# Self-attention of a decoder: the causal mask of the scores by query goes from TensorE into VectorE's maximum

## The chip, the cores and the metric

The kernel runs on one core of a Trainium2 chip. Its time is the device time of one execution in microseconds. The engines are named as in the profile: PE is TensorE (PEld its weight loads), DVE VectorE, ACT ScalarE, POOL GpSimd, SP SyncE. DVE, ACT and PE reach PSUM[...].

## The reference

A decoder of two layers over x of shape (4, 512, 512): in each layer a self-attention, a cross-attention (in the second layer, a mix with a learned adjacency) and a feed-forward part, each with a residual and a layer norm after it. The change lies in the two self-attentions, 16 heads of 32:

```python
scores = jnp.einsum('bhqd,bhkd->bhqk', q, k) * scale
causal = jnp.tril(jnp.ones((S, S), dtype=bool))
scores = jnp.where(causal, scores, jnp.float32(-jnp.inf))
attn = jax.nn.softmax(scores, axis=-1)
out = jnp.einsum('bhqk,bhkd->bhqd', attn, v)
```

## The kernel before

The program runs in stages: the self-attention of layer 0 (to about 640 us of the span), the cross-attention with the quantisation of the weights behind it, the feed-forward part of layer 0, the self-attention of layer 1 (about 1490 to 2110 us), the adjacency and the experts.

**Two sets of scores.** `self_attention` works on groups n of four heads: 4 batches x 4 groups = 16 a layer. It forms the scores twice. `maxima` (L226) has queries on the partitions: for one block of 128 queries, i, and each of the four heads r, PE multiplies the queries with the first m = i + 1 blocks of keys (L237), four heads side by side on their own 32 rows of the array. The last block of keys is the one on the diagonal, and there PE adds the causal mask by a second product, the 128 x 128 bf16 mask times the identity, into the same PSUM tile (L243). DVE then takes the maximum of two heads in one instruction and writes it negated into `st` (L245). `parts` (L250) splits the negated maxima into three bf16 pieces in `pm`; `least` (L258) turns them over on PE (the rows `tp<-ident,pm`) and ACT copies them out. `softmax` (L270) has keys on the partitions: PE forms the scores again, adds the negated maxima with `pick` and the mask (rows `sc<-ident,mask`, L289, which the change leaves alone), and ACT takes the exponential. `values` (L294) sums the exponentials with `ones` (tile `tp`), multiplies them with the values (tile `mm`), and DVE forms four reciprocals `u` (L312) and the product `oT` (L313). `output` (L315) multiplies with Wo, and DVE adds it to x and normalises (L327 to L340).

**The loop** (L356) has 64 + 6 steps a layer. Step t = 4n + m calls, in this order: `maxima(n, 3 - m)`, so that the widths are 512, 384, 256 and 128 columns at m = 0, 1, 2, 3; `least` of the group before at m = 0; the first half of a dense piece (a projection of the next batch: q at m = 2, k at m = 3, v at m = 0); the `softmax` of five steps earlier; the second half of the dense piece. At m = 1 the dense piece is `values` and comes whole behind the softmax. In the last batch, from step 54, there are no projections left. `output` of a finished batch runs in four pieces over the following steps, and one step of the background (the selection of the adjacency: DVE, ACT, POOL and a little of PE) is put in at the end of each.

**What sets the order.** PE's matmuls of the attention are chained in program order by `in_order` (L395); a scheduler places all else on each engine when the program is built. So PE stands still when the next product of the chain isn't free to run. What frees it are PSUM tiles: `psum(3, 1, 1)` gives three pairs of banks for scores, one `tp` and one `mm`. `maxima` takes two pairs (heads 0 and 1, heads 2 and 3), `softmax` two more, from a ring of three. So the second pair of a softmax is the first pair of the maxima of the same step, and its products wait until DVE has read heads 0 and 1. The one `mm` tile goes from projection to projection and to `values`: the k products wait until DVE has read qT out of it (L214), the v products for ACT's kT (L218), the q products at m = 2 for oT.

Of the kernel before, what the change touches and what calls it, by code (L numbers as in the profile page):

```python
# [13 lines left out]
F32 = mybir.dt.float32  # L14
BF16 = mybir.dt.bfloat16
U32 = mybir.dt.uint32
AF = mybir.ActivationFunctionType
ALU = mybir.AluOpType
AX = mybir.AxisListType
PSUM = bass.MemoryType.PSUM  # L20

P = 128
B, S, D = 4, 512, 512
NT = S // P
# [4 lines left out]
NEG = -1e30  # L29
LOWEST = -3.4028235e38  # L30
# [10 lines left out]
def decoder_kernel(ctx: ExitStack, tc: tile.TileContext, a: dict, out: bass.AP):  # L41
    nc = tc.nc
    V, A, G, T = nc.vector, nc.scalar, nc.gpsimd, nc.tensor
# [14 lines left out]
    def psum_pair():  # L58
        return ps["sc"].tile([P, 2, 512], F32, tag="sc", name="sc")

    def psum_tp(dt=F32, n=4):
        return ps["tp"].tile([P, n, P], dt, tag="tp", name="tp")

    def psum_mm():
        return ps["mm"].tile([P, 512], F32, tag="mm", name="mm")
# [4 lines left out]
    ident16 = const.tile([P, P], BF16, tag="ident16", name="ident16")  # L70
    make_identity(nc, ident16)
    mask16 = const.tile([P, P], BF16, tag="mask16", name="mask16")
# [63 lines left out]
    def self_attention(pre, first, background=lambda: None):  # L136
        HD, NG, NJ = 32, 4, 4
        scale = 1.0 / math.sqrt(HD)
        multiply, transpose = in_order()
        with tc.tile_pool(name=pre + "w", bufs=1) as wp, tc.tile_pool(  # L140
            name=pre + "qkv", bufs=2
# [21 lines left out]
                G.memset(pick[32 * r : 32 * r + 3, r, :], 1.0)  # L163

            PM = []
            VA = []
            for k in range(2):
                t = wp.tile([P, NT, NJ, 32], BF16, tag=f"pm{k}", name=f"pm{k}")
                G.memset(t, 0.0)
                PM.append(t)  # L170
                t = wp.tile([P, NT, 4 * NG, HD], F32, tag=f"va{k}", name=f"va{k}")
                VA.append(t)
            XT, Q, K, ST, NM, O = {}, {}, {}, {}, {}, {}
# [19 lines left out]
            def project(b, f, k):  # L193
# [25 lines left out]
                else:  # L219
                    V.tensor_tensor(  # L220
                        VA[b % 2][:, f], pp.rearrange("p (h e) -> p h e", e=HD),
                        bias["v"].rearrange("p (h e) -> p h e", e=HD), ALU.add,
# [3 lines left out]
            def maxima(n, i):  # L226

                b, g = divmod(n, NG)
                if n not in ST:
                    ST[n] = po.tile([P, NT, NJ], F32, tag="st", name="st")  # L230
                st = ST[n]
                m = i + 1
                sc = [psum_pair() for _ in range(NJ // 2)]
                at = [sc[r // 2][:, r % 2, : m * P] for r in range(NJ)]
                for r in range(NJ):
                    rows = slice(HD * r, HD * (r + 1))
                    multiply(  # L237
                        at[r], Q[b][rows, g, ts(i, P)], K[b][rows, g, : m * P],
                        start=True, stop=False,
                    )  # L240
                for r in range(NJ):

                    multiply(at[r][:, i * P :], ident16, mask16, start=False, stop=True)  # L243
                for h in range(NJ // 2):
                    V.tensor_reduce(  # L245
                        st[:, i, 2 * h : 2 * h + 2], sc[h][:, :, : m * P], AX.X, ALU.max,
                        negate=True,
                    )

            def parts(n):  # L250
                st, pm = ST[n], PM[n % 2]
                rest = po.tile([P, NT, NJ], F32, tag="rest", name="rest")
                V.tensor_copy(pm[:, :, :, 0], st)
                V.tensor_tensor(rest, st, pm[:, :, :, 0], ALU.subtract)
                V.tensor_copy(pm[:, :, :, 1], rest)
                V.tensor_tensor(pm[:, :, :, 2], rest, pm[:, :, :, 1], ALU.subtract)

            def least(n):  # L258

                tp = psum_tp(BF16)  # L260
                for i in range(NT):
                    transpose(
                        tp[:, i, :], PM[n % 2][:, i].rearrange("p j e -> p (j e)"), ident16
                    )
# [29 lines left out]
            def values(n):  # L294

                b, g = divmod(n, NG)
                o, t = psum_mm(), psum_tp().rearrange("p n t -> p (n t)")
                for to, left in ((t, None), (o, VA[b % 2])):
                    for kb in range(NT):
# [15 lines left out]
            def output(b):  # L315

                x = X[b]
                st = small.tile([P, NT, 6], F32, tag="bst", name="bst")
                mv = small.tile([P, NT, 2], F32, tag="bmv", name="bmv")
                for i in range(NT):  # L320
                    pw = psum_tp().rearrange("p n t -> p (n t)")
                    for c in range(NK):
                        multiply(
                            pw, O[b][:, c, ts(i, P)], w["o"][:, c, :],
                            start=(c == 0), stop=(c == NK - 1),
                        )
                    V.tensor_tensor(x[:, i, :], pw, x[:, i, :], ALU.add)  # L327
                    V.bn_stats(st[:, i, :], x[:, i, :])
                    V.bn_aggr(mv[:, i, :], st[:, i, :])
                    if i < NT - 1:  # L330
                        yield
                sd = small.tile([P, NT], F32, tag="bsd", name="bsd")
                A.activation(sd, mv[:, :, 1], AF.Sqrt, bias=eps_t)
                rs = small.tile([P, NT], F32, tag="brs", name="brs")
                V.reciprocal(rs, sd)
                for i in range(NT):
                    V.tensor_scalar(
                        x[:, i, :], x[:, i, :], mv[:, i, 0:1], rs[:, i : i + 1],
                        ALU.subtract, ALU.mult,
                    )  # L340
                    yield
# [13 lines left out]
            late = iter(())  # L355
            for t in range(NT * total + 6):  # L356
                n, m = divmod(t, NT)
                k = t - 5
                if n < total:
                    maxima(n, NT - 1 - m)  # L360
# [26 lines left out]
                if m == NT - 1 and n < total:  # L387
                    parts(n)
                if m == 1 and n > 1 and (n - 2) % NG == NG - 1:
                    late = output((n - 2) // NG)  # L390
# [4 lines left out]
    def in_order():  # L395

        last = []

        def pinned(op):
            def call(*args, **kw):  # L400
                ins = op(*args, **kw)  # L401
                if last:
                    tc.add_manual_dep(ins.ins, last[0].name, ORDER, reason="in_order")
                last[:] = [ins.ins]

            return call

        return pinned(T.matmul), pinned(T.transpose)
# [42 lines left out]
    def cross_attention(background):  # L451
        HD, NG, NJ, NP = XD, XG, 4, XP
        multiply, transpose = in_order()
        with tc.tile_pool(name="ck", bufs=1) as kp, tc.tile_pool(
# [6 lines left out]
            G.memset(zero, 0.0)  # L461
            KS, KL, VA, XL = [], [], [], []
            for k in range(2):
# [3 lines left out]
                V.memset(t, 1.0)  # L467
                VA.append(t)
            for k in range(3):
# [4 lines left out]
            def load(b):  # L474
# [6 lines left out]
                G.tensor_copy(  # L481
                    VA[b % 2][:, :, :, :HD], cv.rearrange("p t (g e) -> p t g e", e=HD)
                )
# [891 lines left out]
    with tc.tile_pool(name="sims", bufs=1) as mp:  # L1375
        selection, background = selecting((0, 1), mp, split_context(mp))
        with psum(3, 1, 1):
            self_attention("L0", True, background)
            for _ in selection:
                pass  # L1380
# [17 lines left out]
    with tc.tile_pool(name="sims2", bufs=1) as mp:  # L1398
        selection, background = selecting((2, 3), mp)
        with psum(3, 1, 1):  # L1400
            self_attention("L1", False, background)
            for _ in selection:
                pass
# [49 lines left out]
```

## Time and profile before

| what | number |
| --- | --- |
| time, median of 3 runs | 2757.82 us (2756.66 to 2757.9) |
| the profiled execution's own time | 2759.02 us |
| its span, first to last instruction | 2757.3 us |
| granted TensorE clock, mean over the span | 0.951 |
| PE busy | 2393.0 us, 87% of the span |
| DVE busy | 1412.4 us, 51% |
| ACT busy | 1092.1 us, 40% |
| mask products by query (L243; the row is L401 `sc<-mask,ident`) | 512, mean 228 ns, 52.9 us in all |
| reductions (L245), 1024 / 768 / 512 / 256 elements | 64 of each, mean 1216 / 949 / 682 / 413 ns |
| oT (L313) | 32, mean 690 ns |

A line of the page or of a list names the kernel's line, the engine, the operation, the tile written and those read, partitions x elements, the count, the busy time and the mean of one; behind the second bar stands the engine's idle time ahead of these instructions and what ended it. All products of the attentions carry L401, the line of `in_order`, so they are told apart by their tiles: `sc<-kT,qT` in 32 rows is a score product of `maxima`, `sc<-qT,kT` one of `softmax`. Durations of matmuls overlap, since PE is pipelined; the distance from start to start is what counts.

### The profile page before, as it was taken

How to read it: one execution, taken by the hardware profiler on the slowest of the kernel's cores; microseconds unless marked ns; L12 is line 12 of the kernel's file. 1: busy time of each engine (PE TensorE's matmuls, PEld its weight loads, DVE VectorE, ACT ScalarE, POOL GpSimd, SP SyncE). 2: the span in 40 equal slices, each digit the busy share in tenths (PEclk: the TensorE clock that was granted, in tenths of full speed). 3: DMA queues.
4: the chain of work that ended last, by engine and by line, in shares of the span. 5: the costliest groups of instructions: out<-in, count | busy, mean ns of one | idle time of the engine just before them, and what ended most of it. 6: DMA issues, size and time to landing. Idle time of an engine off the chain costs nothing. (4 is left out here: it accounts for less than half of the span.)

```text
span 2757.3 us, 34743 instructions
## 1 busy us (share of the span) xinstructions
PE 2393.0 (87%) x13465; PEld 1086.1 (39%) x13592; DVE 1412.4 (51%) x2378; ACT 1092.1 (40%) x1706; POOL 623.4 (23%) x1212
## 2 busy tenths in 40 slices
PE   6999989877989899988895899989986897999995
PEld 2344434433333233365553344434442342444442
DVE  0444444447787878678884444444443662111117
ACT  0532272225767677656662622272222330111121
POOL 6300030004333333066764400040000004000004
PEclk9899999998999999999997999999988898999997
DMA  6400000008030401000002000000001005344535
GB/s 219 124 1 20 1 1 1 1 25 311 32 122 24 130 9 39 1 1 1 1 1 75 4 1 1 1 1 1 1 1 57 8 1 202 123 125 142 175 111 182
DMA packets 89879, 156.92 MB, mean 57 GB/s; under 512 B 7152, under 2 KB 39280, under 8 KB 89712
## 3 DMA queue, kind: packets, MB, share of 16 engines
q1 hardware_dynamic: 72304, 115.86, 13.1%
q10 hardware_dynamic: 12288, 22.03, 2.2%
q0 software_dynamic: 5120, 16.78, 1.8%
q8 instruction: 107, 1.75, 0.3%
q14 instruction: 60, 0.49, 0.1%
HBM read 161.99 MB, written 47.71 MB: 76 GB/s over the span
## 5 line engine op out<-in xcount | busy, mean ns | idle before, releaser
L292 ACT ACTIVATE p<-sc 128x512 f32<-128x512 f32 (+3 forms) x256 | 165.9, 700 | 516.5 <-PE sc L401 516.4
L531 DVE TENSOR_REDUCE nm<-sc 128x2 f32<-128x1024 f32 x256 | 304.2, 1218 | 99.0 <-PE sc L401 91.1
L569 ACT ACTIVATE p<-sc 128x1024 f32<-128x1024 f32 x256 | 248.5, 1024 | 135.5 <-PE sc L401 135.4
L245 DVE TENSOR_REDUCE st<-sc 128x2 f32<-128x1024 f32 (+3 forms) x256 | 198.5, 815 | 145.1 <-PE sc L401 144.8
L401 PE MATMUL mm<-p,va 128*32 128x512 f32 (+3 forms) x2048 | 216.3, 527 | 0.5 <-ACT oT L584 0.3
L1318 PE MATMUL sc<-wug,xbT 128*128 128x512 f32 x384 | 186.6, 602 | 12.8 <-issue 7.0
L401 PE MATMUL sc<-qs,ks 128*128 128x512 bf16 x511 | 149.2, 384 | 32.8 <-DVE nm L531 27.4
L401 PE MATMUL sc<-qT,kT 32*128 32x256 f32 (+3 forms) x1024 | 148.5, 500 | 30.8 <-DVE st L245 28.5
L312 DVE RECIPROCAL u<-tp 128x128 f32<-128x128 f32 x128 | 109.8, 914 | 113.5 <-PE tp L401 113.5
L401 PE MATMUL sc<-kT,qT 32*128 32x512 f32 (+3 forms) x1024 | 135.2, 498 | 16.0 <-ACT p L292 11.3
L401 PE MATMUL sc<-ks,qs 128*128 128x512 bf16 x450 | 143.5, 392 | 3.0 <-DVE nm L531 2.3
L977 ACT ACTIVATE junk<-sim,mid 128x512 bf16<-128x512 f32 x176 | 124.6, 719 | 16.6 <-POOL mid L970 16.6
L1345 POOL DMA_INDIRECT yg<-ys,pi x32 | 33.5, 1048 | 387.7 <-DMA ys<-yb 363.4
L722 POOL TENSOR_TENSOR y<-z 128x512 f32<-128x512 f32 (+1 forms) x48 | 97.3, 2040 | 87.3 <-DVE z L707 87.3
L401 PEld LDWEIGHTS sc<-qT,kT 32*128 32x128 f32 x1024 | 57.8, 189 | 117.4 <-issue 55.4
L1325 DVE TENSOR_TENSOR h<-sc,sl 128x256 f32<-128x256 f32 x48 | 20.2, 421 | 163.4 <-ACT sl L1323 163.4
L1183 PE MATMUL sc<-swd,sh 128*128 128x512 f32 x128 | 70.5, 687 | 37.8 <-DVE sh L1178 37.1
L1318 PEld LDWEIGHTS sc<-wug,xbT 128*128 128x128 f32 x384 | 68.8, 192 | 83.3 <-issue 75.7
L722 POOL TENSOR_TENSOR z<-y 128x512 f32<-128x512 f32 x64 | 95.2, 1507 | 3.4 <-issue 2.1
L401 PE MATMUL sc<-nmT,pick 128*128 128x256 bf16 (+3 forms) x480 | 89.7, 309 | 5.6 <-issue 5.6
L1332 PE MATMUL sc<-wd,hT 128*128 128x512 f32 x192 | 94.0, 613 | 0.0
L401 PEld LDWEIGHTS sc<-kT,qT 32*128 32x128 f32 x1024 | 52.7, 191 | 101.3 <-issue 69.9
(295 smaller groups left out, 4239.9 us busy)
## 6 DMA issues: line engine op xcount, KB each, us to landing
wug<-in_Wu SPq DMA_DIRECT2D x48, 512.0 KB
wug<-in_Wg SPq DMA_DIRECT2D x48, 512.0 KB
wd<-in_Wd SPq DMA_DIRECT2D x48, 512.0 KB
xs<-zero SPq DMA_DIRECT2D x3, 4096.0 KB
xb<-xs SPq DMA_DIRECT2D x48, 256.0 KB
ys<-yb ACTq DMA_DIRECT2D x48, 256.0 KB
w<-in_w_gate SPq DMA_DIRECT2D x16, 512.0 KB
w<-in_w_up SPq DMA_DIRECT2D x16, 512.0 KB
```

The costliest lines, as they stand in the source:

```text
L245: V.tensor_reduce(st[:, i, 2 * h : 2 * h + 2], sc[h][:, :, : m * P], AX.X, ALU.max, negate=True,)
L292: A.activation(heads, sc[h][:, :, :m], AF.Exp)
L312: V.reciprocal(u[:, ts(i, P)], t[:, ts(i, P)])
L401: ins = op(*args, **kw)
L531: V.tensor_reduce(NM[n][:, i, 2 * h : 2 * h + 2], sc, AX.X, ALU.max, negate=True)
L569: A.activation(p[:, 2 * h : 2 * h + 2, :], sc[h], AF.Exp)
L722: then(pool, getattr(G, op)(*args))
L977: A.activation(e, s[k], AF.Sign, bias=bias[:, k : k + 1], accum_out=to[:, k : k + 1])
L1183: T.matmul(po[:, i, :], h[:, f, ts(2 * k + i, P)], swd[:, half * (F // P) + f, :], start=(f == 0), stop=(f == F // P - 1),)
L1318: T.matmul(pp[:, 0, :], xbT[:, c, :], wug[s][:, c, :, :].rearrange("p q f -> p (q f)"), start=(c == 0), stop=(c == NK - 1),)
L1332: T.matmul(pp[:, 1, :], hT[:, c, :], wd[s][:, c, :], start=(c == 0), stop=(c == F // P - 1),)
L1345: G.indirect_dma_start(out=y, out_offset=None, in_=ys, in_offset=bass.IndirectOffsetOnAxis(pos[k][:, t : t + 1], 0),)
```

## The change

Each layer makes one more tile, `late_keys`, 128 x 512 fp32: zero in the first 384 columns and the causal mask in the last 128. The mask products by query are gone. For each head, one VectorE instruction (`tensor_tensor_reduce`) reads that head's scores from PSUM and the last m blocks of `late_keys` from SBUF, adds them, writes the sum in bf16 to a tile `e` that nothing reads (two buffers), and its maximum goes to `st`. It is followed by an instruction of its own that writes the accumulator out; both stand on DVE's queue. So a step has four instructions with four accumulator writes, in place of two reductions. The maximum is no longer negated, and `parts` turns the sign in its first two instructions. The softmax's own mask by key stays on PE.

```diff
             PM = []
+            late_keys = wp.tile([P, S], F32, tag="late", name="late_keys")
+            G.memset(late_keys, 0.0)
+            make_causal_mask(nc, late_keys[:, S - P :], NEG)
             VA = []
...
                     multiply(
                         at[r], Q[b][rows, g, ts(i, P)], K[b][rows, g, : m * P],
-                        start=True, stop=False,
+                        start=True, stop=True,
                     )
                 for r in range(NJ):
 
-                    multiply(at[r][:, i * P :], ident16, mask16, start=False, stop=True)
-                for h in range(NJ // 2):
-                    V.tensor_reduce(
-                        st[:, i, 2 * h : 2 * h + 2], sc[h][:, :, : m * P], AX.X, ALU.max,
-                        negate=True,
+                    e = po.tile([P, m * P], BF16, tag="e", name="e")
+                    V.tensor_tensor_reduce(
+                        e, at[r], late_keys[:, (NT - m) * P :], 1.0, LOWEST, ALU.add, ALU.max,
+                        accum_out=st[:, i, r : r + 1],
                     )
 
             def parts(n):
                 st, pm = ST[n], PM[n % 2]
                 rest = po.tile([P, NT, NJ], F32, tag="rest", name="rest")
-                V.tensor_copy(pm[:, :, :, 0], st)
-                V.tensor_tensor(rest, st, pm[:, :, :, 0], ALU.subtract)
+                V.tensor_scalar(pm[:, :, :, 0], st, -1.0, None, ALU.mult)
+                V.scalar_tensor_tensor(
+                    rest, st, -1.0, pm[:, :, :, 0], ALU.mult, ALU.subtract
+                )
                 V.tensor_copy(pm[:, :, :, 1], rest)
                 V.tensor_tensor(pm[:, :, :, 2], rest, pm[:, :, :, 1], ALU.subtract)
```

In the built program the four products of `maxima` and everything else on PE keep their order, but for a few products of the background. On DVE the new instructions stand where the reductions stood, with one difference that comes back in nearly every group with values: the first of the four instructions at m = 2 stands between the four reciprocals and oT, where both reductions stood behind oT.

## The prediction

> **What bounds the kernel now.** I read the busy time by stage first. Only the two self-attentions change (70 to 570 us and 1560 to 2090 us):
>
> ```profile
> 70.00:570.00 500.00, 456.80 (x3019) 202.40 (x3030) 229.98 (x379) 175.14 (x358) 48.08 (x256) 0.96 0.07 20
> 1560.00:2090.00 530.00, 481.26 (x3319) 218.44 (x3334) 237.38 (x389) 170.78 (x321) 46.88 (x182) 0.95 0.00 1
> ```
>
> The columns are the length, then busy time of PE, weight loads, DVE, ACT and POOL, the granted clock, DMA. PE is busy 91% of both, DVE 46%. So PE sets the pace, and what DVE does counts only where PE waits for it. The waits of the first stage say where that is:
>
> ```profile
> PEld sc L401 <- DVE st L245: 28.2, 26, 5.6
> PE sc L401 <- DVE st L245: 17.3, 22, 5.4
> PEld mm L401 <- DVE oT L313: 15.4, 11, 2.0
> PE mm L401 <- DVE oT L313: 13.1, 10, 1.8
> ```
>
> Total us, times, longest. PE already waits 17 us for the maxima and 13 us for oT, once in each of some 11 groups (1.3 us each). The timeline shows one group of four steps (start, duration, engine, line; in brackets the idle time before and who ended it):
>
> ```profile
> 303.00 0.75 DVE L214 TENSOR_SCALAR qT<-mm,L0bq 128x512 f32<-128x512 f32 x1 [4.49 <-PE mm L401]
> 303.32 0.40 PE L401 MATMUL sc<-mask,ident 128*128 128x128 bf16 x4
> 303.80 0.30 PEld L401 LDWEIGHTS mm<-xt,L0wk 128*128 128x128 f32 x2 [0.26 <-DVE qT L214]
> ...
> 310.83 0.40 PE L401 MATMUL sc<-mask,ident 128*128 128x128 bf16 x4
> 311.06 0.39 PE L401 MATMUL tp<-ident,pm 128*128 128x128 bf16 x4
> ...
> 315.91 0.93 PE L401 MATMUL sc<-kT,qT 32*128 32x384 f32 x8
> 316.01 0.69 DVE L220 TENSOR_TENSOR va<-mm,L0bv 128x512 f32<-128x512 f32 x1 [2.51 <-PE mm L401]
> 317.09 1.82 DVE L245 TENSOR_REDUCE st<-sc 128x2 f32<-128x768 f32 x2 [0.38 <-PE sc L401]
> 318.10 0.70 PE L401 MATMUL sc<-qT,kT 32*128 32x256 f32 x4 [0.31 <-DVE st L245]
> ...
> 321.93 3.39 DVE L312 RECIPROCAL u<-tp 128x128 f32<-128x128 f32 x4 [3.02 <-PE tp L401]
> 325.43 0.69 DVE L313 TENSOR_TENSOR oT<-mm,u 128x512 f32<-128x512 f32 x1
> 326.03 1.28 DVE L245 TENSOR_REDUCE st<-sc 128x2 f32<-128x512 f32 x2
> 326.36 1.88 PE L401 MATMUL mm<-xt,L0wq 128*128 128x512 f32 x4
> ```
>
> The reader is to see three gates on PE: qT (303.80), the first half of the maxima (318.10), oT (326.36). Behind each, a PE instruction saved before the gate saves nothing.
>
> **What is removed.** 128 steps (64 in a layer) lose four mask products each. From 310.83 to 311.06 four take 0.23 us of PE's stream. If all counted: 128 x 0.23 = 29 us. They don't, by the step of a group (m = 0, 1, 2, 3 has 512, 384, 256, 128 columns):
> - m=0: no gate near; 0.23 gained.
> - m=3: the next product waits for qT anyway (303.80): 0.
> - m=2: it waits for oT: 0.
> - m=1: it waits for the maxima; see below.
>
> **What is added.** Two reductions become four T(c), the new instruction over one head's c columns, each followed in the built order by a second DVE instruction that writes the accumulator. No row here is either. Nearest for the first: other DVE instructions with two fp32 inputs, 512 elements, 690 ns (TENSOR_TENSOR L313) to 744 (SCALAR_TENSOR_TENSOR L1349). Nearest for the second: ACT's accumulator reads, 196 ns a row, but ACT starts a pass and its read every 0.705 us for a 0.72 row, so the read costs some 0.09 in sequence. One column is 1.04 ns (the reductions grow 267 ns for 256 elements), and 512 of them 533.
>
> Here **a rule of the Trainium skill speaks against the change**: "VectorE: DVE Perf Modes", section "The DRAIN you can't avoid", says the next instruction doesn't start until the pipe is empty, and its rules for kernel authors ask for few instructions. The trace differs: at 928.91 a reduction has a row of 1.18 us and the next one starts at 930.02, 0.07 before its end. By the rule T costs c x 1.04 ns + 0.36 us (744 - 533 + 155 for a 128x1 DVE row); by the rows + 0.23 (744 - 533 - 70 + 90); at best + 0.17 (from 690, rounded up). I take f = 0.23: T(512) 0.76, T(384) 0.63, T(256) 0.50, T(128) 0.36; ends 0.17 and 0.36.
>
> DVE's load grows by 4 x 2.25 - 6.52 (the four pairs of reductions: 2 x (1.216+0.949+0.682+0.413)) = 2.5 us a group, 80 us in all; DVE stays under 60% busy. By place:
> - m=1, 12 steps a layer before the last batch: DVE may start when va ends (316.70) instead of behind the mask (317.09), 0.39 sooner; two T(384) and the read's tail take 1.31 instead of 0.95. Sum -0.03. In two of the 12 the output's normalisation goes ahead of both and the start isn't sooner: +0.35. Total +0.4.
> - m=2: the order as built puts one T(256) between the reciprocals and oT, where the reduction stood behind oT. Its scores are ready (324.6 against 325.3), so oT, and PE's projection behind it, come 0.50 later. 9 groups a layer: +4.5; in 2 more it takes the place of a normalisation (0.45): +0.1.
> - m=0, 12 steps: two T(512) end some 1.57 after 310.9, at 312.5; PE needs them at 312.9. Covered: -0.23 x 12 = -2.8 stays.
> - m=3: T(128) starts behind qT; PE needs it 2 us later. 0.
> - The last batch has no projections to cover DVE (10 steps). Same arithmetic on the waits at 505.20, 521.07, 528.17, 541.84: about +0.35 where x and bn_stats or oT stand ahead, -0.23 where nothing waits. Total +1.5.
> - The first six steps have no softmax between; DVE sets them. Four steps take 9.0 us of DVE for 6.5. In layer 0 PE (at half clock there) hides most: +0.4. In layer 1 DVE also has the selection's work and PE waits 3.3 and 1.7 us for it: +3.
>
> Layers: 2 x (0.4 + 4.5 + 0.1 - 2.8 + 1.5) + 3.4 = **+11 us**. With f = 0.17 the same places give +3.5; with 0.36 +27. The two changed instructions of parts (128x16) keep their count; least reads them 5 us later. The new key mask is two memsets and a select on POOL, about 1 us by the memset rows (0.53 for 512 columns), beside the pm memsets at 3 and 1493 us, over 60 us ahead of its first use: nothing. e has two buffers and no reader; its waits are for DVE instructions long done.
>
> **The clock.** Each oT wait grows from 1.3 to some 2 us. The granted clock reacts to waits of that size:
>
> ```profile
> 265.00:270.00 5.00, 3.16 (x32) 1.48 (x24) 5.00 (x10) 0.00 (x0) 0.00 (x0) 1.00 0.01 2
> ...
> 540.00:545.00 5.00, 3.41 (x18) 1.74 (x16) 3.29 (x7) 0.62 (x1) 0.00 (x0) 0.78 0.00 0
> 545.00:550.00 5.00, 3.70 (x20) 1.72 (x16) 1.57 (x6) 2.18 (x3) 0.00 (x0) 0.50 0.00 0
> ```
>
> An idle 1.8 us at 265 left it at 1.00; 1.6 us at 540 took it to half. The Trainium skill's "TensorE: Matmul & The Clock Gate" (Part 1) lets it fall only after an idle window of some 3.4 us, and by that rule the change costs nothing here; the row says a wait of 1.6 us can do it. A fall costs about half of 3.4 us (that page's window, an estimate), 1.7. Of the 18 groups with the longer wait I count 2 or 3: **+4**; ends 0 and 18 (ten).
>
> **Sum.** 2757.3 + 11 + 4 = 2772 span. The profiled execution took 2759.0, 1.7 over its span, and the median of the runs shown, 2757.8, lies 0.5 over it: 2772 to 2773; I say 2772.
>
> **Rivals.**
> - *Clock falls in half of these groups*: 9 or 10 x 1.7 = +16 instead of +4, 2784; with f = 0.36, 2800. For: 540. Against: 265.
> - *The new waits are hidden, or the cheap end holds* (f = 0.17, no fall): 2761; a little cheaper still and it is within 0.2% of before. For: DVE's 54% idle. Against: the built order at oT.
> - *Faster*, PE-bound everywhere: 2757.8 - 29 = 2729 if no gate existed; with the gates it needs f below some 0.06, where T(512) and its read together take less than the 690 ns of a plain TENSOR_TENSOR.
> - *T runs at half rate.* "Vector Engine (DVE) Microarchitecture Reference", section "Points that are easy to get wrong", says the scalar_tensor_tensor shape halves its throughput on two SBUF sources that aren't bf16. L1349 has two fp32 SBUF sources and takes 744 ns for 512: no halving; and here one source is PSUM. If it held, T(512) is 1.3: m=0 loses too, some 37 us a layer, 2831.
>
> **Chances.** Forecast (2763.5 to 2779) 0.50, clock 0.20, hidden 0.15, faster 0.08, half rate 0.07. A measurement of this kernel can tell 0.2% (5.5 us) from no change. Slower: forecast, clock, half rate = 0.77; same 0.15; faster 0.08. The range 2757 to 2797 leaves out the faster case, the half rate and the lower part of the hidden one, 0.2.
>
> **What would show it.** Right: T(512) rows of 690 to 750 ns; DVE 40 us a layer busier; PE's wait for oT near 2 us a group; the waits for maxima 20 us or less per layer; the m=0 step 0.23 shorter. Wrong: accumulator rows well over 0.2 us in sequence, a T(256) that doesn't stand in front of oT in time, or a granted clock under 0.93 in these stages, or over 0.97.

## The result, and the profile after

The changed kernel takes **2742.12 us** (median of 5 runs, 2733.39 to 2747.61) against 2757.82 for the kernel before (5 runs, 2755.21 to 2758.43): ratio **0.9942**, 95% interval 0.9922 to 0.9962. It is 16 us faster, where 15 us slower was forecast. The profiled execution took 2739.32 us, its span is 2737.6, 19.7 shorter than before.

The busy time by stage, of the changed kernel (columns as above; the second stage begins 13 us earlier now, its window 20):

```profile
70.00:570.00 500.00, 442.46 (x2845) 193.96 (x2860) 240.82 (x769) 180.58 (x367) 47.91 (x256) 0.95 0.07 20
1540.00:2070.00 530.00, 468.18 (x3072) 208.09 (x3087) 246.11 (x773) 177.08 (x338) 51.21 (x203) 0.95 0.00 1
```

DVE has grown by 11 and 9 us in these stretches, 18 in the whole span (1412.4 to 1430.8), not by 80. The groups of instructions say why (line, tile, count; busy, mean ns of one; idle time ahead):

```profile
L247 DVE CUSTOM_DVE_ANT_0 e<-sc,late_keys 128x512 bf16<-128x512 f32 x128 | 81.1, 685 | 93.9 <-PE sc L405 93.9
L247 DVE CUSTOM_DVE_ANT_0 e<-sc,late_keys 128x256 bf16<-128x256 f32 x128 | 47.0, 405 | 0.5 <-PE sc L405 0.5
L247 DVE DVE_READ_ACCUMULATOR2_ANT st<- 128x1 f32 x512 | 42.5, 83 | 0.0
```

T(512) has a row of 685 ns, just under the 690 to 744 that the prediction leant on, and the accumulator's read has one of 83. What counts is how they follow each other. The timeline of the changed kernel, a step m=0 and a step m=1 of one group:

```profile
308.56 0.69 DVE L247 CUSTOM_DVE_ANT_0 e<-sc,late_keys 128x512 bf16<-128x512 f32 x1 [5.36 <-PE sc L405]
309.18 0.08 DVE L247 DVE_READ_ACCUMULATOR2_ANT st<- 128x1 f32 x1
309.18 0.69 DVE L247 CUSTOM_DVE_ANT_0 e<-sc,late_keys 128x512 bf16<-128x512 f32 x1
...
313.32 0.93 PE L405 MATMUL sc<-kT,qT 32*128 32x384 f32 x8
...
314.28 0.56 DVE L247 CUSTOM_DVE_ANT_0 e<-sc,late_keys 128x384 bf16<-128x384 f32 x1 [0.16 <-PE sc L405]
...
314.76 0.55 DVE L247 CUSTOM_DVE_ANT_0 e<-sc,late_keys 128x384 bf16<-128x384 f32 x1
315.24 0.08 DVE L247 DVE_READ_ACCUMULATOR2_ANT st<- 128x1 f32 x1
...
315.38 0.70 PE L405 MATMUL sc<-qT,kT 32*128 32x256 f32 x4 [0.71 <-DVE st L247]
```

The second T starts at 309.18, in the same moment as the first one's read and 0.07 before the first row ends. From T to T it takes 0.61 us at 512 columns, 0.48 at 384, 0.345 at 256, 0.215 at 128: in the prediction's terms (512 columns are 533 ns) f is **0.08**, not 0.23. Four heads at the four widths come to 6.6 us a group, as the reductions did (6.52).

At m=2 the built order stood as foreseen, a T(256) ahead of oT. The same group, first in the kernel before, then in the changed one:

```profile
293.12 3.39 DVE L312 RECIPROCAL u<-tp 128x128 f32<-128x128 f32 x4 [3.02 <-PE tp L401]
...
296.62 0.69 DVE L313 TENSOR_TENSOR oT<-mm,u 128x512 f32<-128x512 f32 x1
...
297.37 1.98 PE L401 MATMUL mm<-xt,L0wq 128*128 128x512 f32 x4 [1.18 <-DVE oT L313]
```

```profile
288.96 3.39 DVE L316 RECIPROCAL u<-tp 128x128 f32<-128x128 f32 x4 [2.92 <-PE tp L405]
...
292.27 0.36 DVE L247 CUSTOM_DVE_ANT_0 e<-sc,late_keys 128x256 bf16<-128x256 f32 x1
...
292.55 0.69 DVE L317 TENSOR_TENSOR oT<-mm,u 128x512 f32<-128x512 f32 x1
...
293.39 2.96 PE L405 MATMUL mm<-xt,L0wq 128*128 128x512 f32 x4 [1.70 <-DVE oT L317]
...
296.27 1.56 PE L405 MATMUL sc<-qT,kT 32*128 32x384 f32 x8
```

oT starts only 0.1 us later behind the reciprocals (3.59 instead of 3.50), and PE's projection 0.18 later, counted from the step's first score product. But PE, which no longer has the mask products to do, now idles 1.70 us here (1.18 before), and four projection products take 2.96 us where they took 1.88 to 1.98: the granted clock has fallen. The same stretch in windows:

```profile
290.00:295.00 5.00, 3.30 (x35) 1.55 (x27) 4.27 (x12) 0.00 (x0) 0.00 (x0) 0.92 0.01 3
295.00:300.00 5.00, 5.00 (x22) 1.77 (x20) 0.00 (x0) 1.20 (x2) 0.00 (x0) 0.74 0.00 0
```

0.08 and 0.26 off the clock in 5 us each are 3.4 us at half clock; the step is 1.64 us longer for it. It happened behind oT in 8 groups (in the kernel before in 2). Step by step, by the distance of one step's first score product to the next one's, after less before: in the full groups m=0 -0.22 us, m=1 -0.14, m=2 +0.16 (or +1.8 with a fall of the clock), m=3 0.00. The 64 steps of layer 0 are 11.0 us shorter, those of layer 1 4.5, the stages between 2.9, the tail 1.8; the start is 0.5 later.

### The profile page after: what moved, and what is told of

Same layout as the page of the kernel before. It is cut to its first block, busy times and chain, and to the rows that moved or that the text cites. A ratio compares the mean times of both kernels' runs of the same rounds, so it can differ in the third digit from the quotient of the medians.

```text
span 2737.6 us, 34686 instructions
## 1 busy us (share of the span) xinstructions
PE 2352.1 (86%) x12953; PEld 1061.5 (39%) x13080; DVE 1430.8 (52%) x3146; ACT 1092.0 (40%) x1706; POOL 625.4 (23%) x1218
## 3 DMA queue, kind: packets, MB, share of 16 engines
q8 instruction: 103, 1.69, 0.3%
## 5 line engine op out<-in xcount | busy, mean ns | idle before, releaser
L247 DVE CUSTOM_DVE_ANT_0 e<-sc,late_keys 128x256 bf16<-128x256 f32 (+3 forms) x512 | 222.9, 482 | 119.4 <-PE sc L405 119.3
L405 PE MATMUL mm<-xt,L0wq 128*128 128x512 f32 x128 | 68.5, 666 | 33.0 <-DVE oT L317 14.0
```

Of the source, the lines that this page charges most:

```text
L247: V.tensor_tensor_reduce(e, at[r], late_keys[:, (NT - m) * P :], 1.0, LOWEST, ALU.add, ALU.max, accum_out=st[:, i, r : r + 1],)
```

## The experiments

PRICE is the theory that the prediction failed by what one T costs in DVE's sequence; the rivals put it down to the built order, to the places of the sum, or to the clock. The kernel before ran beside each set, and took 2757.9, 2733.7, 2734.9 or 2735.1 us by the chip, so ratios to it are compared, not times. Most edits bind one DVE instruction behind another (`dep(a, b)`: a behind b; `OT` holds the latest oT instruction); the diffs are shortened to what matters.

**The halves of the change.** First PE's half: the mask products by query are left out, the reductions stay (so the maxima are over unmasked scores, and q is scaled to a tenth, which keeps the exponentials finite).

```diff
-                    multiply(at[r][:, i * P :], ident16, mask16, start=False, stop=True)
...
+                    if h == 0 and i == 1 and OT:
+                        dep(d, OT[0])
```

> The PE part alone: the kernel before without its mask products by query, with its two reductions a step and oT ahead of the reductions as before. The maxima are then taken over unmasked scores, and q is scaled to a tenth so that the exponentials stay finite; the attention's values differ, and with them the experts' routing, so the two self-attention stages are compared step by step. Theory PRICE (one head's new instruction costs DVE 0.61, 0.48, 0.345, 0.215 us from start to start with its read, so no more than the reductions, and the gain is PE's): the same steps as in the changed kernel or a little shorter, m=0 -0.22, m=1 -0.15 to -0.25, m=2 0, m=3 0 against before, some -9 us in 22 full groups, and the whole near 2742. Theory SCHEDULE (the gain comes from other places of background work and of the half clock): no more than -4 us, near 2754.

Measured: 2721.72 us (2718.84 to 2727.4), ratio 0.9868 (0.9848 to 0.9889). Steps (m=0, 1, 2, 3): -0.22, -0.22, 0.00, 0.00. What the prediction called "if all counted", 29 us, is exceeded, though two of the four steps give nothing.

Then DVE's half: T as in the change, with the mask products back on PE.

```diff
+                for r in range(NJ):
+                    multiply(at[r][:, i * P :], ident16, mask16, start=False, stop=True)
```

> The DVE part alone: the changed kernel with the mask products by query put back on PE (the mask is added twice). oT stands ahead of the instructions at m=2 in this build. Theory PRICE: DVE is as fast as before, so the time is that of before, 2754 to 2762; a step at m=1 0.05 to 0.15 longer (2 x 0.48 + 0.08 = 1.04 for 0.95), the others alike. My prediction's f = 0.23 would give 2770. Theory SCHEDULE: away from 2758 by over 6 us in either direction, without any step of a full group changed.

Measured: 2765.05 (2761.27 to 2775.15), ratio 1.0035 (1.002 to 1.005). Steps: 0.00, +0.18, 0.00, 0.00. Four single heads in place of two pairs cost 0.18 at the one gate where two of them stand ahead of PE. (In this build oT goes ahead of T at m=2.) The halves add up to -36 + 10 = -27 us, rounded, and the change gave -16. These 11 us are hardly more than the three intervals allow together (some 10); the order at oT, which is that of before in both halves, is one candidate for them.

**The order at oT.** The change with oT ahead of the first T at m=2:

```diff
+                    if r == 0 and i == 1 and OT:
+                        dep(d, OT[0])
```

> The changed kernel with one order added: at m=2 the first of the four instructions stays behind oT. Theory PRICE with the clock as its own cost: the +0.16 at m=2 goes (22 groups, -3.5 us), and if the half-clock windows behind the oT wait (+1.64 each, 8 of 22 groups in the changed kernel's profile) come from that wait's length, some of them go too: 2728 to 2738. If the falls have nothing to do with it: 2736 to 2740. Theory SCHEDULE: no rule, within the spread of the changed kernel's runs, 2733 to 2748.

Measured: 2736.65 (2734.11 to 2738.66), ratio 0.9926 (0.991 to 0.9942), 4 us under the change, with intervals that overlap. The m=2 step goes from +0.16 to 0.00, no ordinary group (one without a normalisation in front of oT) has a fall of the clock at oT, 3 of the 8 falls are left, at waits of over 2 us, and the runs spread over 5 us instead of 14. The same with the mask products kept at m=2 alone, where oT also comes first:

```diff
-                        start=True, stop=True,
+                        start=True, stop=i != 1,
                     )
+                if i == 1:
+                    for r in range(NJ):
+                        multiply(at[r][:, i * P :], ident16, mask16, start=False, stop=True)
```

> The changed kernel with PE's mask products kept at m=2 only, where they lie in the wait for oT (the mask is added twice there); in this build oT also stands ahead of the new instructions. The mask products cost no time there if the gate is real, and PE's idle time in that wait is 0.23 us shorter. Theory PRICE with the clock set by PE's idle time: m=2 as before (0 for +0.16), no or few half-clock windows in these groups, 2726 to 2736, no slower than the kernel with oT first. If PE's products at m=2 are on the path after all: 22 x 0.22 = 5 us slower than that one.

Measured: 2736.66 (2731.27 to 2743.17), ratio 0.9927 (0.9908 to 0.9946); -0.22, -0.14, 0.00, 0.00. The four products that this kernel still makes are free. Whether the falls came of oT's delay or of PE's idle time, the next kernel tells: these mask products, but the T ahead of oT, as in the change.

```diff
+                    if r == 0 and i == 1 and OT:
+                        dep(oT, d)
```

> The changed kernel, with the mask products kept on TensorE at m=2 and the first T(256) put ahead of oT, as it stands in the changed kernel. TensorE's idle time in front of the projection behind oT is then some 0.23 us shorter than in the changed kernel, at the same order on VectorE. IDLE (the half-clock stretches behind the wait for oT come of TensorE's idle time, which the missing products lengthen): m=2 steps +0.1 to +0.2 against before, with no stretch of half clock behind oT in the ordinary groups; 2735 to 2741. ORDER (they come of oT being later, whatever TensorE did ahead of it): m=2 steps +1.8 in some 8 of 22 groups, as in the changed kernel; 2740 to 2750.

Measured: ratio 0.9916 (0.9898 to 0.9934). Its timeline at the place of the fence above:

```profile
292.83 0.36 DVE L251 CUSTOM_DVE_ANT_0 e<-sc,late_keys 128x256 bf16<-128x256 f32 x1
293.12 0.69 DVE L324 TENSOR_TENSOR oT<-mm,u 128x512 f32<-128x512 f32 x1
...
293.95 1.95 PE L416 MATMUL mm<-xt,L0wq 128*128 128x512 f32 x4 [1.37 <-DVE oT L324]
```

The order on DVE and the +0.16 are those of the change, PE idles 1.37 instead of 1.70, and in 11 such groups the clock never fell, where it fell in 6 of 10 in the change. It is the idle time.

T at 512 and 384 columns only, the form of before at 256 and 128:

```diff
-                        start=True, stop=True,
+                        start=True, stop=i > 1,
                     )
+                if i < 2:
+                    ...
+                    return
```

> The changed kernel with T only at 512 and 384 columns; at 256 and 128 the mask products and the pair reductions of the kernel before. Both of these steps end at a gate (oT, qT) that the mask products lie ahead of, and TensorE's idle time in front of the gates is as short as before. STEPS: m=0 -0.22, m=1 -0.14, m=2 and m=3 0.0, no half-clock stretch behind oT: 0.991 to 0.994 of before, like the kernel with the products kept at m=2 alone. If taking the products away at m=3 gains something after all, it is slower than that one by 3 us or more (over 0.9945).

Measured: ratio 0.9935 (0.9914 to 0.9957). The products at m=3 are as free as at m=2. These versions can't be told from each other; they lie at or under the change's ratio.

**The price itself.** Can the forecast be brought back by making T dear? First, a short memset behind each head, with the next T bound behind it:

```diff
+                    f = po.tile([P, 64], BF16, tag="pad", name="pad", bufs=1)
+                    g = V.memset(f, 1.0)
+                    dep(g, d)
```

> The changed kernel, with a VectorE memset of 128x64 bf16 put directly behind each head's instruction (512 in all), so that one costs more in VectorE's sequence, much as the prediction had assumed it to. PRICE (the prediction went wrong because it took 0.23 us over the columns for an instruction and its accumulator read, where the trace shows 0.08; the places where it counts were right): with the memset's some 0.1 to 0.15 us a head back in the sequence, the time comes back to 2756 to 2775, near the 2772 predicted, and the m=2 step of a full group is 0.1 to 0.3 us longer than in the changed kernel, m=1 0.2 to 0.35 longer, m=0 and m=3 unchanged. PLACES (the price matters little; the sum's places were wrong as well, since VectorE has slack there): less than 8 us over the changed kernel's 2742, so under 2750.

Measured: ratio 0.9967 (0.9955 to 0.9979), with m=1 0.02 longer than in the change and all other steps unchanged. It told little: the memset has a row of 0.11 us, and the next T starts 0.02 us behind its start,

```profile
313.25 0.11 DVE L255 MEMSET pad<- 128x64 bf16 x1
313.27 0.63 DVE L248 CUSTOM_DVE_ANT_0 e<-sc,late_keys 128x512 bf16<-128x512 f32 x1
```

so the price was hardly raised. The time, under 2750 in the terms of the first chip, is what PLACES had named, but with the price left as it was it doesn't decide between the two, and the two intervals of the ratios, this one's and the change's, overlap. Then a copy of 128 fp32 columns in the same place, with oT bound behind the first T and its copy:

```diff
+                    g = V.tensor_copy(e[:, :P], late_keys[:, :P])
+                    dep(g, d)
```

> The changed kernel with a VectorE copy of 128x128 fp32 behind each head's instruction (the memset of the earlier run went by in 0.02 us and so tested little); oT stands behind the first T(256) and its copy. One head then costs some 0.13 us more in VectorE's sequence, 0.21 over its columns in all, near the 0.23 that the prediction took. PRICE (the prediction failed by this term alone): the m=2 step grows by 0.1 to 0.15 over the changed kernel's and m=1 by as much to twice as much, half-clock stretches follow more of the oT waits, the first six steps and the last two groups lose their gain; 10 to 30 us over the changed kernel, 0.998 to 1.005 of before. PLACES (the sum over the places was wrong too): under 0.9965 of before.

Measured: **ratio 1.0149** (1.0126 to 1.0173), 57 us over the change. The timeline of this kernel:

```profile
307.58 0.36 DVE L249 CUSTOM_DVE_ANT_0 e<-sc,late_keys 128x256 bf16<-128x256 f32 x1
...
307.99 0.23 DVE L255 CAST e<-late_keys 128x128 bf16<-128x128 f32 x1
308.13 0.68 DVE L328 TENSOR_TENSOR oT<-mm,u 128x512 f32<-128x512 f32 x1
...
308.96 3.42 PE L420 MATMUL mm<-xt,L0wq 128*128 128x512 f32 x4 [1.95 <-DVE oT L328]
```

The copy writes the tile that T has just written and starts 0.12 behind the read, so from T to T it is now 0.87 us at 512 columns: f = 0.34, more than was aimed at, and close to the dear end of the prediction, 0.36. For that end, with falls in half of the groups, it had said 2800; 1.0149 x 2757.8 is 2799. Steps: -0.22, +0.12, +0.41 (+2.05 in 10 groups with a fall), 0.00. That the two figures agree to 1 us is luck: the interval is 6 us either way, and m=2 grew by 0.41 where this f gives 0.61 in the prediction's arithmetic. It also lies over the 0.998 to 1.005 that PRICE had named for f = 0.21. But with the order of the change kept, the dearer head turns 16 us of gain into 41 of loss. So PRICE holds for the sign.

**The selection.** The steps account for some 9 us of gain at the places (worked out in the next section), and the falls at oT took 13 back (5 when those that went elsewhere are counted). The rest had to lie elsewhere, so the selection was taken out of the attentions' steps, in the kernel before, in the change, and in the change with oT first:

```diff
-            self_attention("L0", True, background)
+            self_attention("L0", True)
...
-            self_attention("L1", False, background)
+            self_attention("L1", False)
```

> The kernel before, with the selection of experts no longer interleaved into the two self-attentions (its steps run when the attention has ended). It is slower than before by what the interleaving hides, some 60 to 250 us. It is the base for the next kernel. No theory is told apart by it alone.

> The changed kernel, with the selection no longer interleaved, to be compared with the kernel before with the same edit. STEPS (the gain is made in the attention's own steps: m=0 -0.22, m=1 -0.14, m=2 +0.16 with the first groups and the last batch besides): the difference of the two is 5 to 9 us. BACKGROUND (a good part of the 16 us is gained where VectorE's work of the selection stands between the steps, which has room now): 5 us or less. CLOCK (the rest is where the half-clock stretches happen to lie): 10 us or more, with other positions than with the interleaving.

> The changed kernel with oT ahead of the first T(256), and with the selection no longer interleaved; to be compared with the kernel before with the selection taken out of the attentions in the same way. In 12 full groups a layer m=0 -0.22, m=1 -0.14, m=2 0.0, m=3 0.0, and in the last two groups of a layer -1.7. STEPS (with the order mended, the steps alone show): the sum is 2 x (12 x 0.36 + 1.7) = 12 us less than that kernel, less 2 to 4 us that the first six steps give back: 8 to 12 us, and no half-clock stretch behind an oT wait. CLOCK (half-clock stretches come wherever they come, whatever the order at oT): 4 us or less, as with the changed kernel's order, where it was 2.

> The kernel before with the selection no longer interleaved, once more, as the base of the run above on the same chip: 1.0407 to 1.045 times before, as measured.

> The kernel before without the mask products by query (its maxima are over unmasked scores, q is scaled to a tenth, oT is kept ahead of the reductions), with the selection no longer interleaved. Its steps in the full groups should be -0.23, -0.23, 0.0, 0.0 and the last two groups -1.8 or so: 2 x (12 x 0.46 + 1.8) = 15 us under the kernel before with the selection taken out, which was 1.0428 of before twice: 1.037 to 1.038. SELECTION (the further 20 us that this edit gained with the selection interleaved, 36 in all, came of how the selection's work lies between the steps): 1.036 to 1.039. ATTENTION (they were gained in the attention's own steps): 1.033 or less.

> The changed kernel with the mask products kept on TensorE, with the selection no longer interleaved. In the full groups m=1 +0.17 and the others 0.0, and some +3 in the last groups: 5 to 10 us over the kernel before with the selection taken out (1.0428): 1.044 to 1.047. SELECTION (this half of the change gains nothing where the selection is interleaved): the same +0.35% or so that it cost with the selection, 1.045 to 1.047. GRAIN (single heads gain where the selection's instructions stand on VectorE's queue, since these can go between them): its cost without the selection is 8 us or more above its cost of 10 with it, over 1.049.

The last two are the halves of the change. All of them against the kernel before:

```
                      selection interleaved   selection taken out   less 1.0428
before                1                       1.0428 (twice)         -
the change            0.9942                  1.0407                -0.0021
the change, oT first  0.9926                  1.0379                -0.0049
PE's half             0.9868                  1.0338                -0.0090
DVE's half            1.0035                  1.0485                +0.0057
```

Each ratio has an interval of about 0.002 either way. Without the selection the steps of the full groups are the same to 0.02 us (-0.22, -0.14, +0.15, 0.00), the falls at oT come as with the selection (at 6 of the 18 waits of 1.7 us or more), and the change gains 2 us between the medians on one chip (2848.47 against 2850.48) and 5 between the means; with oT first it gains 11.7 (2840.52 against 2852.26), and there the 16 waits of 1.5 us had no fall, though 3 of the 4 longer ones had. The 2 us are fewer than the 5 to 9 that STEPS expected, and within what BACKGROUND had named; with oT first the 8 to 12 of STEPS are met. With the selection interleaved each of the four edits comes out 0.0022 to 0.0042 better, 6 to 12 us. That is the size of the error of one such difference (some 0.0035), and the four share one base, so the gain is likely and its size is not settled. Neither half explains it alone, and the last two runs fell between what the theories expected of them.

Where it lies in the profiled runs can be seen: in layer 0, groups 1 to 3 (5.5 us more than their steps' due, with the fall of the clock taken off) and group 9 (4.2 us in all). One such place, first in the kernel before, then in the changed one:

```profile
391.50 0.69 DVE L999 SCALAR_TENSOR_TENSOR y<-y,sim 128x512 f32<-128x512 f32 x1 [0.69 <-ACT y L998]
392.12 2.35 DVE L245 TENSOR_REDUCE st<-sc 128x2 f32<-128x1024 f32 x2
...
393.39 0.80 PE L401 MATMUL sc<-qT,kT 32*128 32x128 f32 x4 [5.44 <-DVE st L245]
```

```profile
384.68 0.69 DVE L1003 SCALAR_TENSOR_TENSOR y<-y,sim 128x512 f32<-128x512 f32 x1
385.29 0.68 DVE L247 CUSTOM_DVE_ANT_0 e<-sc,late_keys 128x512 bf16<-128x512 f32 x1
...
386.65 0.80 PE L405 MATMUL sc<-qT,kT 32*128 32x128 f32 x4 [2.37 <-DVE st L247]
```

Before, the reductions stood behind a second round of the selection, which itself waits for ACT, and PE for all of them, 5.44 us. In the changed build two T went ahead of that round. This isn't T's doing: with DVE's half alone the longest wait for the maxima in this stage is 5.3, with PE's half alone 2.4. Nor do the missing mask products alone bring it about, since with T at 512 and 384 columns only it is 4.3. Each build places the selection anew; why this one came out better is not shown.

## Why the prediction was wrong, step by step

- **The price of T** is the step that failed, in size: "by the rows + 0.23 (744 - 533 - 70 + 90); at best + 0.17", where 0.08 was measured. Of its three terms the 744 of another instruction was 59 ns too dear, and the "90 in sequence", carried over from ACT, is 0: the read and the next T start together. The overlap of 70 was right. The range left the truth outside, since "at best" again charged the read. The Trainium skill, "VectorE: DVE Perf Modes", has two sections that bear on it. The prediction weighed only the first, "The DRAIN you can't avoid", without its clause that an instruction which isn't held starts earlier. The second, "Two Vector instructions with no wait between them", lets a following instruction start early unless it is held, and judges an accumulator's read as an instruction of its own by that rule. The trace agrees with the second (309.18 against a row's end at 309.25).
- **m=0** (-0.23, 12 steps): measured -0.22. Right. **m=3** (0): 0.00, and the kernel with T at 512 and 384 only shows that nothing is lost there. Right.
- **m=1** (-0.03): measured -0.14. Two errors met. The prediction let DVE start when va ends; it starts when the scores of its head are ready, 0.96 us behind the first score product (314.28 less 313.32) instead of 0.79. And two T(384) with the wait behind them take 1.10 (315.38 less 314.28), not 1.31.
- **m=2** (+0.50): the order and the gate were right, the size was +0.16. The price explains this down to 0.35 only. The rest: oT had to wait for the last reciprocal anyway and started 0.11 behind its row (296.62, 293.12 + 3.39), while T, which doesn't read `u`, starts 0.08 ahead of that row's end (292.27, 288.96 + 3.39). So of the 0.28 from T to oT 0.19 is hidden. With the copy behind each head it was +0.41.
- **The last batch** (+1.5 a layer): wrong sign, -1.7 in group 15 of layer 0 without the selection. At m=0 of that group (-1.07) nothing stands ahead of DVE, and T starts when its own head's scores are there, 1.17 us after the first of them, where the reductions had to wait for all scores and the mask behind them (2.41). The prediction charged the price and saw no earlier start.
- **The first six steps** (+0.4 and +3): without the selection about +0.7 in layer 1, and in layer 0 +0.2 in the change, -1.1 with oT first.
- **DVE** (+80 us): +18.
- **The clock** (2 or 3 falls in 18 groups, +4): 8 falls of 1.64 behind oT, +13, where the kernel before had 2. The cost of one (1.7) was right, their number was not. But other falls went (group 14 of layer 0 had lost 3.5 us), and between the first and the last step of the two stages the time at half clock grew from 89.5 to 99.0 us, so the net is +4.8 at most. That this is near the +4 is luck.

With 0.08 in its own formula the prediction would have had -8 us for the places (+11 at 0.23, +3.5 at 0.17, on the same line); the measured steps give 2 x (-2.7 - 1.7 + 1.7 - 1.7) = -9. That these agree is partly luck: at 0.08 its arithmetic has -0.33 at m=1 and +0.35 at m=2, and the two misses cancel.

So the price accounts for 19 of the 30 us between forecast and result: with it mended, and +4 for the clock, the forecast is 2754, hardly a change. The change without the selection, 2 to 5 us faster, fits that. The other 12 us or so, from -9 + 4.8 to the measured -16, come in, as far as these runs show, where the selection is interleaved; the prediction has no term for it, and how much of it is order and how much the place of the clock's falls stays open.

The rival "Faster" came nearest. It asked for f below some 0.06, or a T(512) with its read in less than 690 ns; measured were 0.08, and 0.61 us from T to T.

## What to carry to other kernels

Price an instruction by the distance from its start to the next one's in a queue that doesn't wait, and try the sum with the cheapest figure that the rows allow: here the sign hung on 0.15 us, 512 times. Work taken from TensorE ahead of a gate saves nothing there and lengthens its idle time, which can cost more in clock than the work did (here 1.64 us a fall for 0.23 of products): leave it, or bring the gate forward. And where a scheduler interleaves other work, expect a few tenths of a per cent from its new order alone.

## What the hardware showed that was not expected

**The clock has an edge in the idle time.** Over the 16 profiled executions, by PE's idle time ahead of the q projection that waits for oT, and whether the first row of that projection was longer than 2.3 us (1.95 to 1.98 at full clock):

```
idle, us       waits   clock fell
0.3 to 1.1        16        0
1.2              100        0
1.4 to 1.5        69        0
1.7               35       15
1.8               28       13
1.9 to 2.0        13        9
2.2 to 2.8        37       19
3.7 to 4.2         3        3
```

Up to 1.53 us none of 185 fell, from 1.70 on 59 of 116. Which of these fell is a matter of where the wait lies. In each of the traces the granted clock changes on a grid: all changes lie whole multiples of 3.413 us apart, to 0.005. Take, of the stretches between two lines of this grid, the one that holds most of the wait, and PE's idle time in it. With up to 1.69 us the clock fell at the end of that stretch in none of 226 cases, with 1.70 (half of 3.41) in 15 of 27, with 1.73 to 1.89 in 16 of 20, from 1.90 on in all 28. Two waits of 2.18 us in the changed kernel show it. One, from 260.96 to 263.14, lies whole in one stretch; the other, from 1733.31 to 1735.49, is divided (the granted clock is the third figure from the end):

```profile
260.07:263.48 3.41, 1.23 (x21) 0.61 (x10) 3.41 (x9) 0.00 (x0) 0.00 (x0) 1.00 0.00 0
263.48:266.89 3.41, 3.41 (x8) 1.07 (x10) 1.91 (x7) 0.00 (x0) 0.00 (x0) 0.50 0.00 0
...
1731.21:1734.62 3.41, 2.09 (x36) 0.93 (x28) 3.41 (x7) 0.00 (x0) 0.00 (x0) 1.00 0.00 0
1734.62:1738.04 3.42, 2.55 (x12) 0.99 (x12) 3.12 (x12) 0.00 (x0) 0.00 (x0) 1.00 0.00 0
1738.04:1741.45 3.41, 3.41 (x22) 1.60 (x18) 0.36 (x1) 2.19 (x3) 0.00 (x0) 1.00 0.00 0
```

So the 1.70 us of the change lie just on the edge, and the 1.18 of before, 1.37 and 1.51 of the kernels above lie under it. PE's idle time isn't all that counts: in other places less was enough (1.59 us ahead of 541.84, in the kernel before).

The Trainium skill, "TensorE: Matmul & The Clock Gate", Part 1, lets the clock fall after an idle window of some 3.4 us that runs freely. The grid of 3.41 us fits this window; that half of it idle is enough does not follow from the page.

**DVE's instructions overlap** also where they differ: a T starts 0.02 us behind the start of a memset with a row of 0.11, and together with an accumulator's read of 0.08. An instruction that overwrites the tile of the T before it starts 0.12 behind that read.
